# The last stage of a two-layer model: 24 row gathers given at once, and rows fetched back behind the last sequence's gathers

## The chip, the core and the metric

The kernel runs on one core of a Trainium2 chip. The metric is device time in microseconds of one launch. A core has a matrix engine (TensorE, PE in the profile, with its weight loads as PEld), a vector engine (VectorE, DVE), an activation engine (ScalarE, ACT), a general one (GpSimd, POOL) and a queue for transfers (SyncE, SP). Each engine takes its instructions strictly in its own order; between engines they wait on semaphores. Gathers and scatters by an index are issued by POOL, plain transfers by SP (a few by ACT).

## The reference, cut to what matters

The input x has 4 sequences of 1024 tokens of 256 f32. Layer 0 is windowed attention and a top-2-of-8 mixture of SwiGLU experts, layer 1 full attention with a layer norm; they fill the time up to the last stage. That stage is the end of the second mixture, where each expert chooses its tokens:

```python
def _L1_ffn_ref(x, gate_w, experts):            # x: (4, 1024, 256), already normalised
    gate_logits = jnp.einsum('bnd,de->bne', x, gate_w)
    competitive_gates = sinkhorn(gate_logits)   # 8 rounds: over tokens, then over experts
    vals, idx = jax.lax.top_k(jnp.swapaxes(competitive_gates, -1, -2), M)   # M = 128 per expert
    gate_values = jnp.swapaxes(vals, -1, -2)
    routed_indices = jnp.swapaxes(idx, -1, -2)
    b_idx = jnp.arange(B)[:, None, None]
    routed = x[b_idx, routed_indices]
    routed = jnp.transpose(routed, (2, 0, 1, 3))
    outputs = jnp.einsum('ebmd,edf->ebmf', routed, experts)
    outputs = outputs * jnp.transpose(gate_values, (2, 0, 1))[..., None]
    vals_bmed = jnp.transpose(outputs, (1, 2, 0, 3))
    routed_back = jnp.zeros_like(x).at[b_idx, routed_indices].set(vals_bmed)
    return routed_back
```

Its result is added to x. A token can be chosen by several experts; its row is set, not summed, so that one of the experts wins.

## The kernel before, in words

**Which sequence is where.** Sequences 0 to 2 go through the choice of tokens while layer 1's attention still runs; their slots (token, gate) are ready when the last stage begins. Sequence 3 is normalised, gated and chosen in the last stage itself. So the last stage has two strands, whose instructions are laced together by hand.

**Strand one: the experts on sequences 0 to 2.** There are 24 columns, one for each pair of sequence and expert, of 128 slots each. `take_rows` (L1499) gathers the rows of a column from DRAM (`xn_d`) into a tile `xg` (POOL, an indirect transfer; there are 24 buffers). `turned` transposes two columns on PE and copies them out on ACT (`xgT`); four matmuls follow, and ACT scales the result into `yg` (4 buffers), which SP writes to a table `y_d` in DRAM (L1576). `experts_on` (L1536) does this as a generator, `jobs`, two columns at a time, so twelve pairs. It gives ten gathers at first, and then two more in each `turn`, as the pairs go; these are paced, which means that they wait for ACT's newest instruction.

To bring the rows back to their tokens, the kernel finds for each token its row in `y_d`. ACT makes a row of signs for each column (`hot`, `one_sign`), PE adds them up (`sum_signs`), `ranks` turns the sums (ACT copies them to `both`), and `sources` makes the row numbers on DVE (`key`, then `src_row`). `backs` (L1579) then gathers eight tiles of 128 tokens: for sequence 0 they are accumulated into `x` by the transfer itself, for sequences 1 and 2 they land in `yr` and are added on DVE (`add`). `put_on` (L2377) writes the finished `x` tiles of a sequence to the output: sequences 0 and 1 on SP, sequence 2 on SP and ACT.

**Strand two: the choice for sequence 3.** `share_steps` (L1333) is the eight Sinkhorn rounds: DVE sums, PE adds over the partitions, DVE takes the reciprocal (L1350) and scales. A pair of the first strand stands in the order beside these rounds. `choose_parts` (L1364) then finds the 128 best tokens of each expert, eight at a time, in 16 rounds of a maximum and a replacement on DVE (`top_v`, `cur`). After every fourth round a part, a quarter of 32 slots of each expert, is known: `keep` makes `slot_row` (DVE), `slot_tok` and `slot_gate` (ACT) out of a product on PE. `go_on(n)` advances it by n steps.

For each quarter a: `begin` (L2292) gathers its 256 rows into two tiles `xl` (POOL) and has PE spread the tokens; `aim` (L2318) finds on DVE which of the duplicates lose; `make` (L2334) transposes the rows and multiplies them with the experts in strips of 32 slots; `give` (L2354) makes the finished `row` on DVE and scatters it to the output (POOL).

**What sets the order.** `in_line` puts every ACT, DVE and POOL operation of the stage in the order of the program text; PE's order follows `in_turn`, and SP's the text. So the order of the calls in the last stage is the order on each engine, and a waiting instruction holds up everything behind it there. `pair_of_experts` (L2396) is three steps of the choice, one pair of strand one and two rows of signs.

Of the kernel before, what the change touches and what calls it, by code (L numbers as in the profile page):

```python
# [39 lines left out]
def two_layers(  # L40
# [55 lines left out]
    lines = {"scalar": [], "vector": [], "gpsimd": []}  # L96
# [252 lines left out]
    with ExitStack() as lc:  # L349
        wpool = lc.enter_context(tc.tile_pool(name="a0_w", bufs=1))  # L350
        pool = lc.enter_context(tc.tile_pool(name="a0", bufs=2))
# [429 lines left out]
        for i in range(NT + LAG + 2):  # L781
            last, m = i - LAG, i + AHEAD
# [87 lines left out]
    with ExitStack() as lc:  # L870
        wpool = ffn0.enter_context(tc.tile_pool(name="f0_w", bufs=1))
        spool = ffn0.enter_context(tc.tile_pool(name="f0_s", bufs=1))
        pool = ffn0.enter_context(tc.tile_pool(name="f0", bufs=2))
# [383 lines left out]
        for m, (t0, nt, n) in enumerate(order):  # L1257
            ws, b3_t, _ = ahead
# [240 lines left out]
    def take_rows(slots, columns, pool, behind=None):  # L1499

        xgs = []
        for b, n in columns:
            xg = pool.tile([P, D], F32, tag="xg", name="xg", bufs=24)
            got = in_line(
                "gpsimd", nc.gpsimd.indirect_dma_start,
                out=xg[:, :],
                out_offset=None,
                in_=xn_d[b][:, :],
                in_offset=bass.IndirectOffsetOnAxis(ap=slots[2][:, n : n + 1], axis=0),
            )  # L1510
            if behind is not None:
                paced(got.ins, behind)
            xgs.append(xg)
        return xgs

    def turned(xgs, pool, pieces: int = 1):

        ps = one_bank()
        for h, xg in enumerate(xgs):
            for kc in range(2):  # L1520
                c = (2 * h + kc) * P
                turn_on(ps[:, c : c + P], xg[:, kc * P : (kc + 1) * P], ident)
        xgT = pool.tile([P, 4, P], F32, tag="xgT", name="xgT", bufs=3)
        ps = ps.rearrange("p (k t) -> p k t", k=4)
        for k in range(0, 4, 4 // pieces):
            in_line(
                "scalar", nc.scalar.copy,
                xgT[:, k : k + 4 // pieces], ps[:, k : k + 4 // pieces],
            )
        return xgT  # L1530
# [5 lines left out]
    def experts_on(g: int, columns, pool, w_all):  # L1536

        slot_gate = chosen[g, 0][0]
        depth = 10
        xgs = take_rows(chosen[g, 0], columns[:depth], pool)  # L1540

        def turn(m: int):
            xgT = turned(xgs[m : m + 2], pool)
            more = columns[m + depth : m + depth + 2]
            if more:
                xgs.extend(take_rows(chosen[g, 0], more, pool, lines["scalar"][0]))
            return xgT

        ahead = turn(0)
        yield 0  # L1550
        for m in range(0, len(columns), 2):
            xgT = ahead
            if m + 2 < len(columns):
                ahead = turn(m + 2)
                yield m
            ps = one_bank()
            for h in range(2):
                for kc in range(2):
                    mm_on(
                        ps[:, h * D : (h + 1) * D],  # L1560
                        lhsT=xgT[:, 2 * h + kc, :],
                        rhs=w_all[:, (m + h) % E, kc, :],
                        start=(kc == 0),
                        stop=(kc == 1),
                    )
                if h == 0:
                    yield m
            for h in range(2):
                b, e = divmod(m + h, E)
                yg = pool.tile([P, D], F32, tag="yg", name="yg", bufs=4)  # L1570
                in_line(
                    "scalar", nc.scalar.activation,
                    yg, ps[:, h * D : (h + 1) * D], AF.Copy,
                    scale=slot_gate[:, m + h : m + h + 1],
                )
                nc.sync.dma_start(out=slots_of(SEQS[g][b], e, 0, CAP), in_=yg)  # L1576
            yield m

    def backs(b: int, src_row, pool, adds: bool):  # L1579

        rows = []
        for t in range(TB):
            i = b * TB + t
            yr = pool.tile([P, D], F32, tag="yr", name="yr", bufs=2 * TB) if adds else x_t[i]
            in_line(
                "gpsimd", nc.gpsimd.indirect_dma_start,
                out=yr[:, :],
                out_offset=None,
                in_=y_d[b][:, :],
                in_offset=bass.IndirectOffsetOnAxis(ap=src_row[:, t : t + 1], axis=0),  # L1590
                compute_op=ALU.bypass if adds else ALU.add,
            )
            rows.append((x_t[i], yr))
        return rows
# [5 lines left out]
    chosen = {}  # L1600
# [556 lines left out]
    with ExitStack() as lc:  # L2157
# [85 lines left out]
        def sources(both):  # L2243
            key = pool.tile([P, TB, E], F32, tag="key", name="key")
            in_line(
                "vector", nc.vector.tensor_tensor,
                key.rearrange("p t e -> p (t e)"), both[:, TB * E :], both[:, : TB * E], ALU.subtract
            )
            in_line(
                "vector", nc.vector.tensor_tensor,  # L2250
                key, key, expert_no[:, :1].to_broadcast([P, TB, E]), ALU.add,
            )
            src_row = pool.tile([P, TB], I32, tag="src_row", name="src_row")
            in_line("vector", nc.vector.tensor_reduce, src_row, key, AX.X, ALU.max)
            return src_row
# [30 lines left out]
        def go_on(n: int):  # L2286
            for _ in range(n):
                next(choose, None)

        begun, made = {}, {}  # L2290

        def begin(a: int):  # L2292
            slot_tok, slot_row = chosen[1, a][1:]
            xgs = []
            for h in range(2):
                xg = pool.tile([P, 2 * D], F32, tag="xl", name="xl", bufs=6)
                in_line(
                    "gpsimd", nc.gpsimd.indirect_dma_start,
                    out=xg[:, :],
                    out_offset=None,  # L2300
                    in_=xn_d[NB - 1][:, :],
                    in_offset=bass.IndirectOffsetOnAxis(ap=slot_row[:, h : h + 1], axis=0),
                )
                xgs.append(xg)
            ps = one_bank()
            for h in range(2):
                mm_on(
                    ps[:, h * P : (h + 1) * P],
                    lhsT=slot_tok[:, h : h + 1].to_broadcast([P, P]),
                    rhs=ident,  # L2310
                    start=True,
                    stop=True,
                )
            begun[a] = xgs, ps
# [62 lines left out]
        def put_on(b: int, queues):  # L2377
            for t in range(TB):
                i = b * TB + t
                w = queues[t % len(queues)].dma_start(  # L2380
                    out=out_rows[i * P : (i + 1) * P, :], in_=x_t[i]
                )
                tc.add_to_no_dep_group("whole_rows", w.ins)
                for group in groups_out:
                    tc.declare_no_dep(w.ins, group=group, reason="other sequences")

        def begin_ready():
            for a in range(4):
                if (1, a) in chosen and a not in begun:
                    begin(a)  # L2390

        def add(rows):
            for x, yr in rows:
                in_line("vector", nc.vector.tensor_tensor, x, x, yr, ALU.add)
# [1 line left out]
        def pair_of_experts(signs: bool = True):  # L2396
            go_on(3)
            next(jobs, None)
            sum_signs()
            if signs:  # L2400
                one_sign()
            next(jobs, None)
            next(jobs, None)
            if signs:
                one_sign()

        go_on(3)
        sum_signs()
        at = ranks(0)
        go_on(1)  # L2410
        for _ in range(2):
            pair_of_experts()
        backs(0, sources(at), pool, False)
        for _ in range(2):
            pair_of_experts()
        sum_signs()
        at = ranks(1)
        pair_of_experts()
        begin_ready()
        go_on(1)  # L2420
        rows1 = sources(at)
        put_on(0, [nc.sync])
        pair_of_experts()
        aim(0)
        adds1 = backs(1, rows1, pool, True)
        pair_of_experts()
        pair_of_experts()
        make(0)
        begin_ready()
        pair_of_experts(False)  # L2430
        give(0)
        aim(1)
        for _ in jobs:
            pass
        sum_signs()
        make(1)
        at = ranks(2)
        while (1, 2) not in chosen:
            go_on(1)
        begin_ready()  # L2440
        give(1)
        rows2 = sources(at)
        adds2 = backs(2, rows2, pool, True)
        go_on(2)
        aim(2)
        make(2)
        while (1, 3) not in chosen:
            go_on(1)
        begin_ready()
        give(2)  # L2450
        add(adds1)
        put_on(1, [nc.sync])
# [41 lines left out]
```

## Time and profile before

| | |
|---|---|
| three runs | 2206.23, 2200.26, 2199.81 us; median 2200.26 |
| the profiled execution | 2202.66 us, of which the span from the first to the last instruction is 2200.9 |
| mean granted TensorE clock | 0.970 |
| busy share of the span | PE 94%, DVE 61%, ACT 44%, POOL 30% |
| last stage, POOL | 24 gathers `xg`: 14 from 2061.81 us on, pairs at 2085.25, 2093.73, 2102.95, 2107.10 and 2124.48 |
| last stage, POOL, the rest | `x` (accumulating) from 2109.60, `yr` from 2140.92 and 2170.11; `xl` from 2127.05, 2150.91, 2164.91 and 2182.45 |
| last stage, DVE | first maximum of the choice 2095.80; `slot_row` of the quarters 2111.10, 2138.32, 2164.48, 2182.02 |
| last stage, ACT | last `yg` 2159.99 |
| end of the span | 2200.9 |

All times inside the kernel are microseconds from the start of the span, of the profiled execution. In rows of the timeline the first number is the start, the second the duration; what stands in brackets is the idle time of the engine just in front of it and what ended it ("issue": nothing that the profile shows; "remote": a signal that it can't put down to an instruction). SPq is SP's queue of transfers. In rows of waits the three numbers are the total, how often, and the longest. Many helpers record their operations at one line (L103), so rows are told apart by the names of the tiles.

### The profile page before, as it was taken

What the parts mean: (1) busy time and instruction counts of PE and PEld (TensorE: products, weight loads), DVE (VectorE), ACT (ScalarE), POOL (GpSimd) and SP (SyncE); (2) the same over time, 40 slices, a digit from 0 to 9 for tenths busy, and PEclk for the clock granted to TensorE, in tenths of its full rate; (3) what the DMA queues carried; (4) which work ended last, traced back from release to release, by engine and by line L of the source; (5) the groups of instructions that cost most, each with busy time, mean ns of one, the idle gap of its engine ahead of it and who ended that gap; (6) DMA issues with size and microseconds to landing.
All of it is one profiled execution on the core that took longest, in us unless ns stands there. A gap on an engine that the chain in (4) does not pass through costs nothing.

```text
span 2200.9 us, 50595 instructions
## 1 busy us (share of the span) xinstructions
PE 2061.2 (94%) x20050; PEld 1353.7 (62%) x20050; DVE 1333.0 (61%) x2660; ACT 969.6 (44%) x1885; POOL 669.4 (30%) x947
## 2 busy tenths in 40 slices
PE   6999989999999999998899999999999999997674
PEld 4777765556688888874455555555555655554342
DVE  6676654522222222234789787878787878898464
ACT  3554553111122222212156676666666666655351
POOL 2665551243000000012333322314141404033644
PEclk9999999999999999999999999999999999998686
DMA  5111106112266767655162313131313131100344
GB/s 150 53 42 49 54 14 205 37 62 92 73 201 229 232 222 229 211 182 115 50 133 67 79 51 76 49 63 50 78 51 78 51 75 44 51 22 21 101 112 132
DMA packets 205224, 213.68 MB, mean 97 GB/s; under 512 B 87080, under 2 KB 164360, under 8 KB 204988
## 3 DMA queue, kind: packets, MB, share of 16 engines
q1 hardware_dynamic: 181228, 169.00, 27.1%
q0 software_dynamic: 11952, 30.55, 4.9%
q10 hardware_dynamic: 11808, 10.89, 1.4%
q8 instruction: 159, 2.61, 0.5%
q14 instruction: 77, 0.63, 0.1%
HBM read 140.64 MB, written 57.97 MB: 90 GB/s over the span
## 4 chain that ended last, share of the span: by engine, by line
PE 78%; DVE 8%; issue 6%; POOL 3%; DMA 3%; ACT 2%; SPq 1%; ACTq 0%; DVEq 0%; POOLq 0%
PE one L86 36%; PE acc L86 17%; PE two L86 13%; PE two L82 7%; PE misc L82 2%; PE acc L82 2%; DVE tops L1799 2%; DVE tops L1802 1%; POOL xg L103 1%; PE misc L86 1%; POOL yr L2012 1%; DMA yr<-ys_d,slot 1%; DVE top_v L103 1%; DMA w_t<-in_L_ffn_rw_dram 1%; DVE cur L103 1%
## 5 line engine op out<-in xcount | busy, mean ns | idle before, releaser
L1849 ACT ACTIVATE wide<-one 128x512 f32<-128x512 f32 x1024 | 529.6, 603 | 239.4 <-PE one L86 232.8
L1799 DVE TENSOR_REDUCE tops<-two 128x2 f32<-128x1024 f32 x268 | 325.9, 1218 | 84.6 <-PE two L86 79.3
L1802 DVE TENSOR_REDUCE tops<-one 128x1 f32<-128x512 f32 x488 | 311.8, 679 | 0.0
L86 PE MATMUL acc<-wide,v_t 128*32 128x256 f32 x4096 | 276.7, 388 | 0.4 <-issue 0.4
L86 PE MATMUL two<-xbT,w_t 128*128 128x256 f32 (+1 forms) x1280 | 253.6, 356 | 2.0 <-ACT xbT L1186 1.4
L86 PE MATMUL one<-q_st,k_st 64*128 64x512 f32 x1024 | 238.6, 450 | 6.1 <-DVE gates L1324 5.0
L86 PEld LDWEIGHTS two<-xbT,w_t 128*128 128x128 f32 x1280 | 221.6, 190 | 29.5 <-ACT xbT L1186 1.8
L1219 DVE SCALAR_TENSOR_TENSOR glu_b<-two,b_blk,act_b 128x256 f32<-128x256 f32 (+1 forms) x160 | 72.5, 453 | 244.7 <-ACT act_b L1212 244.7
L86 PE MATMUL one<-top_st,minus 64*128 64x512 f32 x1024 | 209.7, 395 | 0.0
L1212 ACT ACTIVATE act_b<-two,b_blk 128x256 f32<-128x256 f32 (+1 forms) x160 | 72.1, 451 | 295.2 <-PE two L86 155.5
L86 PEld LDWEIGHTS acc<-wide,v_t 128*32 128x32 f32 x4096 | 107.7, 109 | 110.8 <-issue 64.0
L86 PE MATMUL one<-k_st,q_st 64*128 64x512 f32 x488 | 168.8, 449 | 3.0 <-DVE ctx L1881 1.2
L86 PEld LDWEIGHTS one<-q_st,k_st 64*128 64x128 f32 x1024 | 101.6, 185 | 95.4 <-ACT wide L1849 35.2
L318 ACT ACTIVATE act<-two,bT 128x512 f32<-128x512 f32 x60 | 41.2, 687 | 264.7 <-PE two L82 259.2
L86 PEld LDWEIGHTS one<-k_st,q_st 64*128 64x128 f32 x488 | 86.4, 184 | 76.9 <-ACT wide L1849 53.3
L2012 POOL DMA_INDIRECT yr<-ys_d,slot x64 | 61.8, 966 | 212.1 <-DMA ys_d<-yb 80.5
L86 PE MATMUL acc<-w_t,glu_b 128*128 128x256 f32 x552 | 125.6, 379 | 0.0
L1269 POOL TENSOR_TENSOR x<-x,sb_b 128x256 f32<-128x256 f32 x32 | 23.3, 727 | 336.2 <-DVE glu_b L1219 336.2
L82 PE MATMUL two<-wide,w_t 128*128 128x512 f32 x256 | 115.1, 603 | 5.8 <-DVE tops L1799 5.0
L648 POOL TENSOR_SCALAR_AFFINE_SELECT pT<-pT 64x512 f32<-64x512 f32 x128 | 84.0, 656 | 115.1 <-ACT pT L638 113.1
L86 PEld LDWEIGHTS acc<-w_t,glu_b 128*128 128x128 f32 x552 | 101.9, 190 | 12.3
L319 DVE SCALAR_TENSOR_TENSOR glu<-two,bT,act 128x512 f32<-128x512 f32 x60 | 44.8, 747 | 102.8 <-ACT act L318 73.4
(395 smaller groups left out, 3341.4 us busy)
## 6 DMA issues: line engine op xcount, KB each, us to landing
w_t<-in_L_ffn_rw_dram SPq DMA_DIRECT2D x120, 512.0 KB
halves<-split SPq DMA_DIRECT2D x64, 256.0 KB
q_st<-halves SPq DMA_DIRECT2D x128, 128.0 KB
k_st<-halves SPq DMA_DIRECT2D x256, 64.0 KB
xb<-xs_d SPq DMA_DIRECT2D x31, 256.0 KB
ys_d<-yb ACTq DMA_DIRECT2D x31, 256.0 KB
xs_d<-zeros SPq DMA_DIRECT2D x5, 1536.0 KB
b_t<-in_L_ffn_rb_dram SPq DMA_DIRECT2D x40, 128.0 KB
```

The lines of the kernel that those rows point to most:

```text
L82: return do(*args, **kw)
L86: done = do(*args, **kw)
L103: done = do(*args, **kw)
L318: nc.scalar.activation(act, ps[0], AF.Silu, bias=bT[0][:, f, e : e + 1])
L319: done = nc.vector.scalar_tensor_tensor(glu[:, f, :], ps[1], bT[1][:, f, e : e + 1], act, ALU.add, ALU.mult)
L648: nc.gpsimd.affine_select(out=part, in_=part, compare_op=ALU.is_ge, fill=0.0, base=0, pattern=[[0, 8], [1, WIN]], channel_multiplier=-1,)
L1212: nc.scalar.activation(act[:, :cols], ps[:, ff * cols : (ff + 1) * cols], AF.Silu, bias=b_blk[0][:, f, n : n + 1],)
L1219: nc.vector.scalar_tensor_tensor(glu[:, f, :cols], ps[:, 512 + ff * cols : 512 + (ff + 1) * cols], b_blk[1][:, f, n : n + 1], act[:, :cols ...
L1799: last = nc.vector.tensor_reduce(tops[:, :, j, kk], whole[0], AX.X, ALU.max)
L1802: last = nc.vector.tensor_reduce(tops[:, hh, j, kk : kk + 1], sc[hh], AX.X, ALU.max)
L1849: newest["scalar"] = nc.scalar.activation(pt[:, hh * 512 : (hh + 1) * 512], sc[hh], AF.Exp).ins
L2012: ga = nc.gpsimd.indirect_dma_start(out=yr[:, :], out_offset=None, in_=ys_d[:, :], in_offset=bass.IndirectOffsetOnAxis(ap=slots[k][:, i : ...
```

## The change

`experts_on` gives all 24 gathers at its start, with no pacing, and `turn` only transposes. `begin_ready`, which began all quarters that were ready, is replaced by `until(a)`, which goes on with the choice until quarter a is known and begins it at once. The calls of the last stage are put in a new order: the row numbers of sequence 0 are found after one pair instead of two, but its rows are fetched back after four pairs and behind the first quarter's `xl` gathers; `aim(0)`, `make(0)` and `give(0)` come earlier against the pairs; the row numbers of sequence 1 are found two pairs after their `ranks` instead of one; `put_on(0)` stands behind one pair more, and `backs(1)` behind the gathers of the second quarter and the scatters of the first. `make(1)` stands in front of the end of the pairs. From the third quarter on, the order is nearly as before.

In the order on the engines this gives: on POOL 24 `xg`, 2 `xl`, 8 `x`, 2 `xl`, 2 scatters, 8 `yr`, then as before. On SP, behind sequence 0's eight `y_d` writes, come four of sequence 1, five tiles of `put_on(0)`, two writes, three tiles, two writes, then sequence 2's eight; before, the eight tiles of `put_on(0)` stood in front of all of sequence 1's and 2's writes.

```diff
@@ experts_on @@
         slot_gate = chosen[g, 0][0]
-        depth = 10
-        xgs = take_rows(chosen[g, 0], columns[:depth], pool)
+        xgs = take_rows(chosen[g, 0], columns, pool)
 
         def turn(m: int):
-            xgT = turned(xgs[m : m + 2], pool)
-            more = columns[m + depth : m + depth + 2]
-            if more:
-                xgs.extend(take_rows(chosen[g, 0], more, pool, lines["scalar"][0]))
-            return xgT
+            return turned(xgs[m : m + 2], pool)
@@ last stage @@
-        def begin_ready():
-            for a in range(4):
-                if (1, a) in chosen and a not in begun:
-                    begin(a)
-
...
+        def until(a: int):
+            while (1, a) not in chosen:
+                go_on(1)
+            begin(a)
+
         go_on(3)
         sum_signs()
         at = ranks(0)
-        go_on(1)
-        for _ in range(2):
+        pair_of_experts()
+        rows0 = sources(at)
+        for _ in range(3):
             pair_of_experts()
-        backs(0, sources(at), pool, False)
-        for _ in range(2):
-            pair_of_experts()
+        until(0)
+        backs(0, rows0, pool, False)
         sum_signs()
         at = ranks(1)
         pair_of_experts()
-        begin_ready()
-        go_on(1)
+        aim(0)
+        pair_of_experts()
         rows1 = sources(at)
+        make(0)
+        pair_of_experts()
         put_on(0, [nc.sync])
-        pair_of_experts()
-        aim(0)
+        until(1)
+        give(0)
         adds1 = backs(1, rows1, pool, True)
         pair_of_experts()
-        pair_of_experts()
-        make(0)
-        begin_ready()
+        aim(1)
         pair_of_experts(False)
-        give(0)
-        aim(1)
+        make(1)
         for _ in jobs:
             pass
         sum_signs()
-        make(1)
         at = ranks(2)
-        while (1, 2) not in chosen:
-            go_on(1)
-        begin_ready()
+        until(2)
         give(1)
         rows2 = sources(at)
         adds2 = backs(2, rows2, pool, True)
         go_on(2)
         aim(2)
         make(2)
-        while (1, 3) not in chosen:
-            go_on(1)
-        begin_ready()
+        until(3)
         give(2)
```

## The prediction

> **What bounds the kernel now.** The page's engine shares come first: PE is busy 94% of the span, but the slices show that this is the mean over stages, and that the last three slices (from 2036 us on) are different. Everything that the diff touches lies there, so the windows of that stretch are the second view.
>
> ```profile
> 2040.00:2080.00 40.00, 25.08 (x122) 13.63 (x122) 21.83 (x61) 11.48 (x22) 27.28 (x46) 0.59 0.41 123
> 2080.00:2120.00 40.00, 28.54 (x139) 16.81 (x138) 28.21 (x65) 23.77 (x36) 16.43 (x14) 0.87 0.32 80
> 2120.00:2160.00 40.00, 28.42 (x159) 18.87 (x160) 19.42 (x42) 15.92 (x29) 18.89 (x19) 0.83 0.53 141
> ```
>
> The columns are the window, its length, and busy time of PE, weight loads, DVE, ACT and POOL, then clock, DMA share and GB/s. No engine is full: DVE has 19.4 of 40 us in the third. Order and waits bind here, so the third view is the waits of DVE and of ACT from 2060 us to the end.
>
> ```profile
> DVE row L103 <- remote: 10.2, 1, 10.2
> DVE slot_row L103 <- PE one L86: 9.5, 2, 7.5
> DVE slot_row L103 <- remote: 6.6, 1, 6.6
> DVE key L103 <- ACT both L103: 5.8, 1, 5.8
> ```
>
> ```profile
> ACT yg L103 <- issue: 18.6, 6, 8.7
> ACT yg L103 <- DMA y_d<-yg: 8.2, 2, 7.6
> ```
>
> Two chains share the stretch. The first is DVE's choosing: the first maximum starts at 2095.80, maxima and replacements go at about 2.54 us a round, and the third quarter's row numbers (slot_row) come at 2164.48. Before that it stands for 5.84 (key of sequence 1), 7.54 (slot_row of the second quarter) and 10.19 us (row of the first quarter). The second chain is the expert pairs, twelve of them, each ended by two yg on ACT: the fourth at 2105.52, the twelfth at 2159.99. Its gaps from there, by the timeline of ACT, are 6.55, 4.15, 14.7, 6.3, 4.4, 4.15, 11.6 and 2.66 us. From 2164.48 to the end at 2200.9 are 36.4 us, in which both programs hold the same instructions in nearly the same order. So the question is when the third quarter's row numbers and the last yg come.
>
> The 14.7 gap is told by the chain of waits:
>
> ```profile
> 2122.58 4.06 DMA x<-y_d,src_row
> 2126.66 0.33 SPq L2380
> 2127.08 0.38 SPq L1576
> 2127.56 4.36 DMA y_d<-yg
> 2132.01 0.47 ACT yg L103
> ```
>
> SP's queue writes sequence 0 out (L2380) as its rows arrive, and sequence 1's first y_d writes stand behind all of it; yg has four buffers, so ACT waits for these writes.
>
> **The change part by part.** *The ten late gathers given at once.* The timeline of POOL:
>
> ```profile
> 2078.26 0.94 POOL L103 DMA_INDIRECT xg<-xn_d,slot_row  x1 [0.30 <-issue]
> 2085.25 0.94 POOL L103 DMA_INDIRECT xg<-xn_d,slot_row  x1 [6.04 <-ACT xgT L103]
> 2086.49 0.95 POOL L103 DMA_INDIRECT xg<-xn_d,slot_row  x1 [0.30 <-issue]
> ```
>
> A gather follows the next at 1.25 us, so ten more take 12.5 us and the burst that starts at 2061.81 ends near 2091.7, not 2079.2. Nobody waits for these rows so early: saved by themselves, 0. What they may cost is the Sinkhorn rounds beside them. Rounds with little wait take 2.1 to 2.6 us (reciprocal to reciprocal, L1350); the two that end at 2075.29 and 2081.69 take 5.04 and 6.40, with DVE waiting 3.5 and 4.9 us for PE, and the second ends 2.5 us after the last gather of the burst. That reads like PE's signals being held while gathers are issued without a pause, from about 10 us into a burst. If all rounds wait until the longer burst is over, the first maximum comes 12.4 us later; if the delay is that of the rows themselves (a cold PE, clock 0.59 there), 0. Below 0 nothing speaks, since the rounds hold the same work. The nearest case is a round at 6.4 us instead of 2.3 for the added stretch, two or three rounds, 7 us for T0; but T0 only reaches the end through DVE's chain, which has slack (next step), while the pairs behind the rounds lose perhaps half. I take 3 us at the end, bounds 0 to 12.4.
>
> The Trainium skill ("DMA: Bandwidth & Descriptors", the section on the anatomy of a GpSimd DMA) gives each such transfer a fixed 2.0 us and its bytes at 436 GB/s, which for 131 KB is an estimated 2.3 us, against the 1.25 us pitch above; by it the burst would last until about 2102 and the cost be nearly twice mine, some 2194 in all. The row decides for the pitch.
>
> *The DVE waits.* The key of sequence 1 moves two pairs behind its ranks, about 8 us, against a wait of 5.84: gone. The row of the first quarter gets make(0) one pair earlier, and stands right behind slot_row of the second quarter; most of its 10.19 goes (PE had its product at 2150.3, and the signal came at 2155.11, 2.0 us after the burst of yr and xl gathers). The 7.54 in front of slot_row goes with the SP wait, since PE's products in front of it stood behind that yg. Sum 5.84 + 7.54 + 10.19 + 2.00 (in front of slot_row 12) = 25.6 us, bounds 15 to 25.6. DVE alone would have the third quarter's row numbers near 2139. It is no longer what is late; the pairs are.
>
> *The pairs.* On SP, in the new order, four of sequence 1's y_d writes stand in front of put_on(0), two behind its fifth row, two behind its eighth. On POOL two gathers of the first quarter (xl) stand in front of the eight accumulating ones, and wait for slot_row of the first quarter, 2111.10 in this trace. Accumulating ones then go at 1.85 us from 2113.8 instead of 2109.60, 4.2 us later, and the last lands near 2131 (4 us each). The seventh pair's writes so go at about 2126, the eighth's near 2132, landing in 1.9 to 4.4 us: the ninth pair is free, the tenth waits until some 2136. Five gaps with no such stall (6.55, 4.15, 6.3, 4.4, 4.15) have a mean of 5.1 us; eight at that are 41, so the last yg comes at 2146.5, with 2 us for the tenth pair's buffers 2148.5, against 2159.99. Gain 11.5, say 12. Bounds: 8, if the 8.7 us wait in front of the eleventh pair (it stands behind make(0) and the burst of yr gathers) comes back behind make(1) by half; 16, if the gaps are those of 4.2 to 4.4. Of the 10 xg gathers taken from POOL's later queue, the last two stood at 2124.48, in front of xl; that is 2.5 us of POOL off, and not on a path.
>
> *The end.* 36.4 us behind slot_row 12 stay: two xl, the scatters, eight yr, the fourth quarter, the adds and the writes have the same order on POOL and SP. Bounds -2 to +2, since the row numbers of the fourth quarter wait 6.62 us there for a PE that had finished at 2175.75, behind the third burst, and this may fall otherwise.
>
> Sum: profiled execution 2202.66, less 12, plus 3: 2193.7. The profiled one is 2.4 us above the median of the runs shown, 2200.26, so 2191. Of this kernel a measurement can tell about 0.3%, 6.6 us, from no change; the gain is 9.
>
> **The rivals.** *The long burst costs nothing.* If the slow rounds come from the cold clock alone, the 3 us go and the pairs run at their short gaps: 2202.66 - 16 - 2.4 = 2184. For it: the accumulating burst of 2109.60 to 2124 held no signal, and early rounds were slow with the clock at 0.5. Against: both slow rounds and the first yg (7.94 us, "remote") were released right behind the last gather.
>
> *The burst holds the rounds in full, and the gain is used up.* T0 comes near 2107 and the first yg near 2094 instead of 2081.81; three gaps of 6 make the fourth pair 2112, 6.3 late. DVE with its slack is at 2150, the last yg at 2154.5: 2202.66 - 12 + 6.3 - 2.4 = 2194.6, about the line of what can be told; 2200 if the wait in front of the eleventh pair is met again.
>
> *Slower: the hold comes in each burst.* The place is POOL's queue from xl of the first quarter on. With T0 at 2107 slot_row comes at 2122.5, and 2 + 8 + 2 gathers go unbroken for 19.8 us, until 2142.3, where before the eight went ahead of it without need of DVE. If this burst holds as the first, signals come at 2144.5, four pairs at 4.2 follow (2161.3), and the 6.3 us of the third burst of before is met in the middle of them: last yg 2167.6, 7.6 behind now, so 2208, and to 2212 with PE at half clock behind each stop (2165.7 to 2193 has 0.5). It decides from a last yg later than 2166.6, and needs T0 beyond some 2105 and a hold in the accumulating burst too. For it: three of the four bursts show a release just behind them. Against: the accumulating one did not.
>
> **How the numbers follow.** The forecast has 0.42, of which 0.10 lies above 2193.7; no cost 0.12; full hold 0.18; slower 0.28. So faster by over 0.3% is 0.44, within it 0.28, slower 0.28. The likeliest case reaches from 2187 (gain 16 at a cost of 3) to 2198 (gain 8 at a cost of 6). The range to hold the time 8 times in 10 goes from 2184 to 2210, leaving out a little below and the worst of the slow case.
>
> **What would show it.** Right: 24 gathers at 1.25 us from 2062 to 2092; the first maximum at 2096 to 2103; no wait of key; four y_d writes ahead of the rows of sequence 0 on SP; the eleventh yg without its 8.7 us; last yg at 2148 to 2152; slot_row of the third quarter 4 us behind it; then 36 us. Wrong: a first maximum behind 2105; waits called remote of over 5 us behind the accumulating gathers; a new wait of ACT's yg for y_d of 5 us or more; or a last part that is not 36 us long.

## The result, and the profile after

The changed kernel takes 2212.14 us (median of 20 runs, 2199.76 to 2220.74) beside 2200.72 of the kernel before (20 runs, 2195.48 to 2206.68). The ratio is 1.0049, 95% interval 1.0034 to 1.0064: slower by half a per cent, where 2191 was forecast. The profiled execution took 2217.37 us, with a span of 2215.6.

The windows of the last stage of the changed kernel, with the columns as before:

```profile
2040.00:2080.00 40.00, 24.54 (x140) 13.40 (x139) 21.98 (x58) 14.17 (x28) 28.80 (x55) 0.62 0.35 109
2080.00:2120.00 40.00, 19.62 (x76) 11.66 (x75) 14.48 (x50) 10.15 (x14) 13.27 (x14) 0.62 0.21 63
2120.00:2160.00 40.00, 30.90 (x201) 19.58 (x200) 30.19 (x55) 26.12 (x43) 20.68 (x17) 0.93 0.55 136
2160.00:2216.00 56.00, 25.87 (x195) 14.48 (x193) 25.66 (x61) 7.99 (x20) 23.21 (x24) 0.65 0.38 119
```

The window from 2080 to 2120 us is the one that went wrong: DVE is busy for 14.5 us instead of 28.2, ACT for 10.2 instead of 23.8. The third window is the fuller one now (DVE 30.2 instead of 19.4). So something new stops the stage early, and the new order does make the middle denser. The waits of DVE and ACT from 2060 us on name the stop:

```profile
DVE rc L1350 <- remote: 17.5, 2, 11.2
DVE slot_row L103 <- PE one L86: 16.8, 2, 11.7
DVE slot_row L103 <- remote: 6.7, 1, 6.7
```

```profile
ACT yg L103 <- remote: 22.1, 1, 22.1
ACT yg L103 <- issue: 17.0, 6, 4.2
```

In the kernel before, the same two views have these lines for rc and for the first yg:

```profile
DVE rc L1350 <- PE two L86: 8.4, 2, 4.9
ACT yg L103 <- remote: 7.9, 1, 7.9
```

The 5.8 us of key, the 10.2 of row and the 8.2 of yg for its y_d writes are gone, as the forecast had it. In their place stand 17.5 us in front of the Sinkhorn reciprocal rc (instead of 8.4) and 22.1 in front of the first yg (instead of 7.9), both "remote". The timeline of DVE and of POOL puts them beside the gathers:

```profile
2081.08 0.21 DVE L1350 RECIPROCAL rc<-one 128x8 f32<-128x8 f32 x1 [3.76 <-PE two L86]
2093.82 0.21 DVE L1350 RECIPROCAL rc<-one 128x8 f32<-128x8 f32 x1 [11.22 <-remote]
2101.60 0.21 DVE L1350 RECIPROCAL rc<-one 128x8 f32<-128x8 f32 x1 [6.27 <-remote]
```

```profile
2067.43 1.13 POOL L103 DMA_INDIRECT xg<-xn_d,slot_row  x1 [6.16 <-PE misc L82]
...
2096.50 0.95 POOL L103 DMA_INDIRECT xg<-xn_d,slot_row  x1 [0.30 <-issue]
```

The 24 gathers last from 2067.43 to 2097.45, 1.25 us apart. Three rounds in a row are stopped in that time; the last goes on 4.2 us behind the end of the burst, and then rounds take 2.6 to 3.5 us again. The product that the second of them waits for is written down as started on PE at 2082.74, so that DVE had it 11 us after PE began. The page "Perfetto Trace Analysis" of the Trainium skill says (in its part on the lifecycle of an instruction) that the profile's end of a PE instruction is an estimate and not observed. So the trace can't tell whether PE finished late or its signal came late; what counts here is when DVE and ACT could start. "Held" below means no more than that.

Of the 14.7 us between the spans of the two profiled executions, 5.6 lie in front of the stage (the first xg at 2067.43 instead of 2061.81). A second profile of the same changed program (r_after below) has it at 2061.81 again, so these are not of the change. The rest is 13.5 us more between the first xg and the first maximum (47.5 instead of 34.0), 4.9 less from there to the third quarter's row numbers (63.8 instead of 68.7), and 0.4 more from there to the end.

### The profile page after: what moved, and what is told of

Read it like the earlier page. It is cut to its first block, busy times and chain, and to the rows that moved or that the text cites. A ratio compares the mean times of both kernels' runs of the same rounds, so it can differ in the third digit from the quotient of the medians.

```text
span 2215.6 us, 50582 instructions
## 1 busy us (share of the span) xinstructions
PE 2067.6 (93%) x20050; PEld 1356.7 (61%) x20050; DVE 1332.4 (60%) x2660; ACT 969.4 (44%) x1885; POOL 670.3 (30%) x947
## 5 line engine op out<-in xcount | busy, mean ns | idle before, releaser
L86 PEld LDWEIGHTS acc<-wide,v_t 128*32 128x32 f32 x4096 | 107.6, 109 | 110.6 <-issue 63.8
L86 PEld LDWEIGHTS acc<-w_t,glu_b 128*128 128x128 f32 x552 | 101.9, 190 | 12.3
```

The costliest lines, as they stand in the source:

```text
L86: done = do(*args, **kw)
```

## The experiments

The theory that the experiments start from, H: a long, unbroken series of gathers issued by GpSimd holds PE's products back from DVE and ACT, and the change made the series longer. Against it stand the new order itself (O), the bytes that land (B), and the mere number of gathers (N).

The experiments ran in five jobs on four chips: e1 to e4 on one, r_after and e5 on a second, e1b to e4b on a third, e6 and e7 on the first of these again, e6b and r2_after on a fourth. Which chip gave the result above isn't known. The kernel before ran in each job as the yardstick (16 to 35 runs, beside 4 to 12 of a variant), and a ratio is always one to its runs in the same job. It isn't exactly the quotient of the two medians beside it; the two differ by up to 0.0014.

| run | edit, against the kernel named | before, same chip | this | ratio (95%) |
|---|---|---|---|---|
| e1_paced | changed, pacing of before | 2186.18 | 2180.27 | 0.9977 (0.9964 to 0.9991) |
| e2_all24 | before, all 24 at once | 2186.18 | 2184.80 | 0.9992 (0.9980 to 1.0005) |
| e3_rate | changed, spaced xg | 2186.18 | 2182.82 | 0.9991 (0.9978 to 1.0003) |
| e4_plain | changed, plain loads on SP | 2186.18 | 2183.36 | 0.9991 (0.9976 to 1.0006) |
| r_after | changed, unedited | 2200.38 | 2202.42 | 1.0019 (1.0003 to 1.0035) |
| e5_depth4 | changed, paced, four at first | 2200.38 | 2194.76 | 0.9988 (0.9972 to 1.0003) |
| e1b_paced | as e1 | 2199.99 | 2195.97 | 0.9984 (0.9971 to 0.9998) |
| e2b_all24 | as e2 | 2199.99 | 2210.34 | 1.0039 (1.0024 to 1.0054) |
| e3b_rate | as e3 | 2199.99 | 2191.84 | 0.9949 (0.9931 to 0.9968) |
| e4b_plain | as e4 | 2199.99 | 2190.00 | 0.9944 (0.9924 to 0.9964) |
| e6_all_rate | changed, spaced xg and yr | 2183.87 | 2184.91 | 1.0002 (0.9989 to 1.0016) |
| e7_old_rate | before, all 24 at once, spaced | 2183.87 | 2189.62 | 1.0016 (1.0003 to 1.0030) |
| e6b_all_rate | as e6 | 2198.91 | 2186.65 | 0.9947 (0.9928 to 0.9966) |
| r2_after | changed, unedited | 2198.91 | 2203.37 | 1.0023 (1.0010 to 1.0035) |

To read the traces side by side, the last stage is cut in three: A from the last gates (the start of Sinkhorn) to the first maximum, B from there to the third quarter's slot_row, C from there to the end of the span. All are differences of starts in the timeline of DVE. "Held" is the longest wait for rc.

| trace | kernel before there | A | B | C | held |
|---|---|---|---|---|---|
| before | 2200.7 | 29.0 | 68.7 | 36.5 | 4.9 |
| changed | 2200.7 | 42.5 | 63.8 | 36.8 | 11.2 |
| r_after | 2200.4 | 40.2 | 57.8 | 36.3 | 13.2 |
| r2_after | 2198.9 | 40.2 | 58.5 | 36.6 | 11.0 |
| e2b_all24 | 2200.0 | 40.3 | 64.6 | 36.4 | 11.8 |
| e1b_paced | 2200.0 | 27.2 | 65.3 | 36.5 | 5.5 |
| e5_depth4 | 2200.4 | 20.2 | 68.3 | 36.6 | 0.9 |
| e3b_rate | 2200.0 | 20.9 | 66.2 | 36.7 | 0.9 |
| e4b_plain | 2200.0 | 20.2 | 63.2 | 39.7 | 0.9 |
| e6b_all_rate | 2198.9 | 21.0 | 61.7 | 37.4 | 1.0 |
| e2_all24 | 2186.2 | 21.6 | 64.0 | 34.3 | 1.9 |
| e1_paced | 2186.2 | 20.4 | 57.9 | 34.0 | 0.9 |
| e3_rate | 2186.2 | 21.0 | 57.9 | 34.1 | 0.9 |
| e4_plain | 2186.2 | 21.4 | 57.1 | 37.1 | 1.9 |
| e6_all_rate | 2183.9 | 21.2 | 55.8 | 37.3 | 1.8 |
| e7_old_rate | 2183.9 | 21.0 | 65.4 | 34.1 | 0.9 |

**e1_paced: the new order without the long burst.**

```diff
-        xgs = take_rows(chosen[g, 0], columns, pool)
+        depth = 10
+        xgs = take_rows(chosen[g, 0], columns[:depth], pool)
         def turn(m: int):
-            return turned(xgs[m : m + 2], pool)
+            xgT = turned(xgs[m : m + 2], pool)
+            more = columns[m + depth : m + depth + 2]
+            if more:
+                xgs.extend(take_rows(chosen[g, 0], more, pool, lines["scalar"][0]))
+            return xgT
```

> The changed kernel with the gathers of before: ten at first, then two per pair, paced behind ACT; the new order of the last stage stays. Theory H (the longer unbroken burst of gathers holds PE's signals): from the first xg to the first maximum 34 us as before (47.5 in the changed kernel), first yg 20 us behind the first xg (34.2), and the whole near 2195, since the new order by itself gained 4.4 us between the first maximum and the end. Rival O (the new order of the calls makes the choice start late, or gains nothing): 45 us or more to the first maximum, or 34 us and a whole of 2200 or more.

**e2_all24: the long burst without the new order.** The kernel before, with the two lines of the change in `experts_on` alone.

> The kernel before, with only one edit: all 24 gathers given at once, no pacing; the old order stays. Theory H: 45 to 50 us from the first xg to the first maximum, and since the old order gets nothing back, 2209 to 2214. Rival O: 34 us, 2200 within 3.

**e3_rate: the burst longer, but not back to back.**

```diff
                 paced(got.ins, behind)
+            rest = pool.tile([P, 512], I32, tag="rest", name="rest", bufs=1)
+            in_line("gpsimd", nc.gpsimd.iota, rest, pattern=[[1, 512]], base=0, channel_multiplier=0)
             xgs.append(xg)
```

> The changed kernel with a GpSimd iota of 128x512 behind each of the 24 gathers, so that they go at some 2 us instead of 1.25: the burst is longer (about 48 us instead of 30) but not back to back. Theory H in its form 'the rate is the cause' (the accumulating gathers at 1.85 us held no signal): no wait of rc above 4 us, first maximum 32 to 36 us behind the first xg, whole 2195 to 2203. Rival N (the number of gathers under way, or the length of the burst, is the cause): the rounds wait until the 48 us are over, first maximum 50 to 60 us, whole 2220 or more.

**e4_plain: the same bytes by another issuer.** The loads bring rows 128e to 128e+127 instead of the chosen ones, so this kernel leaves out the gather by index.

```diff
-            got = in_line(
-                "gpsimd", nc.gpsimd.indirect_dma_start,
...
-            )
+            e = n % E
+            nc.sync.dma_start(out=xg, in_=xn_d[b][e * P : (e + 1) * P, :])
```

> The changed kernel with the 24 gathers by index replaced by 24 plain loads of the same size on SP (rows 128e to 128e+127 of the sequence instead of the chosen ones, so the experts work on other rows). Theory H (GpSimd's issuing is the cause): no wait of rc above 3 us, first maximum 30 to 34 us behind the first load, whole 2190 to 2198. Rival B (the bytes and the landing of 24 tiles are the cause): waits of rc as in the changed kernel while the loads land, though shorter, and a whole of 2205 or more.

These four ran on one chip, and there the expectation for e2 failed: 21.6 us in A and not the 40 or more that H asked for, with 24 gathers 1.25 us apart just as in the changed kernel. Its rounds:

```profile
2071.33 0.21 DVE L1350 RECIPROCAL rc<-one 128x8 f32<-128x8 f32 x1 [0.91 <-PE one L86]
2074.71 0.21 DVE L1350 RECIPROCAL rc<-one 128x8 f32<-128x8 f32 x1 [1.86 <-PE one L86]
2077.05 0.21 DVE L1350 RECIPROCAL rc<-one 128x8 f32<-128x8 f32 x1 [0.82 <-PE one L86]
```

No wait called remote is in any trace of that chip, and the kernel before was itself 14.5 us faster there. The times that the four expectations name were worked out for the chip of the result and are all too long here; so are their first maxima (25.4 us behind the first xg in e1 and 26.0 in e3, where 34 and 32 to 36 were expected). Either H was wrong, or the hold is there on some chips and not on others. So the next job took the changed kernel unedited, and one with a short series.

**r_after, r2_after: the changed kernel, unedited.**

> The changed kernel once more, unedited, beside the kernel before. The first four experiments showed no wait called remote at all, and the kernel before at 2186 instead of 2200.7, so the hold of PE's signals seems not to be there in every place where the program runs. Theory C (the hold belongs to the chip or session, not to the program): where the kernel before takes some 2186, the changed one shows no rc wait above 3 us, 25 to 28 us from the first xg to the first maximum, and 2180 to 2185, so faster by 0.1 to 0.3%; where the kernel before takes some 2200, 47 us and 2209 to 2215. Rival P (the hold belongs to this program's instruction layout, the four variants having changed it by chance): 45 us or more and 8 us or more behind the kernel before, wherever it runs.

> The changed kernel, unedited, once more. Theory C: if the kernel before takes some 2186 here, no wait of rc above 4 us, the first maximum 26 to 28 us behind the first xg, and 0.996 to 0.999; if it takes some 2200, 45 to 48 us to the first maximum and 1.001 to 1.006. Rival P: the same 45 us or more in either case.

Both met chips on which the kernel before takes some 2200, and both times the hold was there: A 40.2 us, and 1.0019 and 1.0023 (2202.42 us in the first, where 2209 to 2215 was expected). The regression is smaller than the 1.0049 of the first chip, but each interval lies above one.

**e5_depth4: four gathers at first.** As e1, with depth = 4.

> The new order with pacing, four gathers at first instead of ten, then two per pair. Theory H: with a burst of 8 (four, and two pairs in the first turns) no rc wait above 3 us, the first maximum 24 to 27 us behind the first xg, whichever the place, and 1 to 3 us less than the kernel with ten (0.996 to 0.998 of the kernel before where that takes 2186; 0.994 or less where it takes 2200). Rival G (the rows come too late with so few ahead): the transposes wait for xg, yg pairs 2 to 5 later by 4 us each, the same as the kernel before or slower.

On the chip of r_after, a series of at most eight with pauses has A at 20.2 us, as low as on the chip without a hold: 20 us less than the changed kernel, and H's expectation. But B is 68.3, and the tenth and eleventh yg pairs come 12.3 and 10.0 us behind those in front of them. The last four late gathers now stand on POOL behind the eight accumulating ones, from 2127.13 on, and PE's transposes for the tenth pair wait for their rows:

```profile
2131.51 1.09 PE L86 MATMUL one<-ident,xg 128*128 128x128 f32 x4 [4.04 <-DMA xg<-xn_d,slot_row]
```

So rival G is part of it, at the tenth pair and not at the second to fifth; what keeps the eleventh the trace doesn't say. Only 7.7 us of the 20 reach the end; the ratio is 0.9988, within noise of one, where 0.994 or less was expected, and no better than the 0.9984 of ten at first (e1b below).

**e1b, e2b, e3b, e4b: the first four on a chip with the hold.**

> The new order with ten gathers at first and the rest paced, once more, to have it on a chip where PE's signals are held (the kernel before at some 2200 there). Theory H there: as in the kernel before, two rounds are held, the first maximum is 33 to 35 us behind the first xg (45 to 47 with all 24 at once, 25 with four), no gain from the new order that the later bursts don't take back in part: 0.993 to 0.998 of the kernel before. Rival O (the new order itself costs time): 1.000 or more. If the kernel before takes some 2186, 0.997 again and no wait called remote.

> The old order with all 24 gathers at once, once more. Theory H where signals are held: 44 to 48 us from the first xg to the first maximum and 1.004 to 1.008 of the kernel before, since nothing is given back. Rival O: 34 us and 1.000. If the kernel before takes some 2186: 0.999 again.

> The changed kernel with a GpSimd iota behind each of the 24 gathers (1.7 us apart, as the first run of it showed), once more. Theory H, form 'rate': where signals are held no more than one round waits over 3 us, the first maximum 26 to 34 us behind the first xg, 0.993 to 0.998 of the kernel before. Rival N (a long series of gathers, at whatever rate): 45 us or more to the first maximum, and 1.002 or more. If the kernel before takes some 2186: 0.999 again.

> The changed kernel with plain loads on SP in place of the 24 gathers (the experts work on other rows), once more. Theory H (gathers that GpSimd issues): where signals are held, no rc wait above 3 us, first maximum 25 to 28 us behind the gates, later waits behind the yr gathers as in the changed kernel; 0.993 to 0.998 of the kernel before. Rival B (the bytes that land): rc waits of 5 us or more while the loads land, and 1.000 or more. If the kernel before takes some 2186: 0.999 again.

This decides it. First the rounds of e2b, the same program as e2, in the timeline of DVE:

```profile
2073.67 0.21 DVE L1350 RECIPROCAL rc<-one 128x8 f32<-128x8 f32 x1 [1.46 <-PE one L86]
2082.80 0.21 DVE L1350 RECIPROCAL rc<-one 128x8 f32<-128x8 f32 x1 [7.61 <-remote]
2096.13 0.21 DVE L1350 RECIPROCAL rc<-one 128x8 f32<-128x8 f32 x1 [11.81 <-remote]
2098.41 0.21 DVE L1350 RECIPROCAL rc<-one 128x8 f32<-128x8 f32 x1 [0.75 <-PE one L86]
```

One program, two chips: A 21.6 and 40.3 us, ratio 0.9992 and 1.0039. The long burst alone, in the old order, costs 0.39%; theory P (an accident of this program's layout) and rival O fall. Then e3b, where the gathers take longer, 2061.57 to 2101.70, but are 1.71 us apart:

```profile
2061.57 1.12 POOL L103 DMA_INDIRECT xg<-xn_d,slot_row  x1 [6.17 <-PE misc L82]
2062.72 0.58 POOL L103 IOTA rest<- 128x512 int32 x1
2063.46 0.97 POOL L103 DMA_INDIRECT xg<-xn_d,slot_row  x1 [0.17 <-issue]
```

```profile
2072.37 0.21 DVE L1350 RECIPROCAL rc<-one 128x8 f32<-128x8 f32 x1 [0.90 <-PE one L86]
2074.81 0.21 DVE L1350 RECIPROCAL rc<-one 128x8 f32<-128x8 f32 x1 [0.93 <-PE two L86]
2076.88 0.21 DVE L1350 RECIPROCAL rc<-one 128x8 f32<-128x8 f32 x1 [0.54 <-PE one L86]
```

No round waits a microsecond, A is 20.9, and the kernel is at 0.9949, faster than both. Number and length (N) are not the cause; the rate is, and 0.46 us more between two gathers is enough (whether it is the time or the other instruction between them that counts was not told apart). The bytes (B) are not either: e4b, where SP issues the loads, has A 20.2 and 0.9944, and there the transfers moved 220 GB/s from 2065 to 2075 us, against 105 in e2b from 2070 to 2080. But its loads are given within 12 us, less than the 13 us that the series in e2b goes before the first long stop, and they read rows in one piece and not by an index; a longer series of them was not run. Pacing with ten at first (e1b) leaves two slow rounds, as in the kernel before: 32.2 us from the first xg to the first maximum (33 to 35 expected) and 0.9984, a smaller gain than the 0.993 to 0.998 expected.

**e6_all_rate, e6b_all_rate: the yr gathers spaced too.**

```diff
+            if adds:
+                rest = pool.tile([P, 512], I32, tag="rest", name="rest", bufs=1)
+                in_line(
+                    "gpsimd", nc.gpsimd.iota, rest, pattern=[[1, 512]], base=0, channel_multiplier=0
+                )
             rows.append((x_t[i], yr))
```

> The changed kernel with the iota behind each of the 24 gathers and behind each of the 16 yr gathers too (1.7 us apart instead of 1.25; the accumulating ones stay at 1.85). Theory H where the kernel before takes some 2200: the wait called remote in front of the fourth quarter's slot_row (6.5 us in seven of seven traces with held signals) falls below 3, the pairs beside the first yr series go at 4 to 5 us, and the whole is 0.988 to 0.994 of the kernel before. Rival Z (what holds these is the transfers, not the rate of issuing): the remote wait stays at 6 us or grows with the series by 3.6, and 0.995 to 0.998. Where the kernel before takes some 2186, 0.996 to 1.000, since 3.6 us of later yr gathers are paid for nothing.

> The changed kernel with the iota behind each of the 24 xg and the 16 yr gathers, once more, to meet a chip where signals are held (the kernel before at some 2200). Theory H there: the remote wait in front of the fourth quarter's slot_row below 3 us (6.5 in every trace with held signals so far), third quarter's slot_row 58 to 62 us behind the first maximum (66.2 without the yr spacing), 0.986 to 0.993 of the kernel before. Rival Z (the order is worth no more): 64 us or more and 0.994 to 0.998. If the kernel before takes some 2186: 1.000 again.

The fourth quarter's slot_row in e3b and in e6b, both where signals are held:

```profile
2171.33 0.16 DVE L103 CAST slot_row<-one 128x2 int32<-128x2 f32 x1 [6.54 <-remote]
```

```profile
2157.46 0.16 DVE L103 CAST slot_row<-one 128x2 int32<-128x2 f32 x1 [0.36 <-PE one L86]
```

The remote wait of 6.5 us is gone with the spacing, in this series as in the first, and B goes from 66.2 to 61.7. The changed kernel without spacing (r2_after) ran on the same chip in the same job: A 40.2 against 21.0, ratio 1.0023 against 0.9947. The fourth and fifth rounds there, first in r2_after, then in e6b:

```profile
2081.82 0.21 DVE L1350 RECIPROCAL rc<-one 128x8 f32<-128x8 f32 x1 [8.30 <-remote]
2094.44 0.21 DVE L1350 RECIPROCAL rc<-one 128x8 f32<-128x8 f32 x1 [11.04 <-remote]
```

```profile
2071.75 0.21 DVE L1350 RECIPROCAL rc<-one 128x8 f32<-128x8 f32 x1 [1.01 <-PE two L86]
2073.81 0.21 DVE L1350 RECIPROCAL rc<-one 128x8 f32<-128x8 f32 x1 [0.54 <-PE one L86]
```

But the 0.9947 is no better than e3b's 0.9949 on another chip: part of what spacing gives is paid for by the longer series, C 37.4 instead of 36.7 here, 37.3 instead of 34.1 where nothing is held. On the chip without a hold the version is at 1.0002. The expected 0.986 to 0.993 was not met; only the mechanism was.

**e7_old_rate: what the new order is worth.** As e2, with e3's iota.

> The kernel before, in its old order, with all 24 gathers given at once and the iota behind each: what the new order is worth by itself, when the gathers hold nothing. The forecast's step said that the new order takes 12 us from the way between the first maximum and the third quarter's row numbers (68.7 us in the kernel before). Expected if that was right: the first maximum 26 us behind the first xg, 67 to 70 us from there to the third quarter's row numbers, and some 8 to 12 us slower than the new order with the same iota (e3: 66.2 us where signals are held). Rival W (the new order gains little): within 4 us of it.

On the chip without a hold B is 65.4 us in the old order (67 to 70 expected) and 57.9 in the new (e3): 7.5 us. The ratios, 1.0016 and 0.9991, each 0.0013 either way, put the new order at 0.25%, some 5.5 us: less than the 8 to 12 expected and more than the 4 of rival W. e1 against its yardstick, where both pace their gathers, gives 0.23%, some 5 us. So the order is a gain. The spacing itself isn't free where nothing is held: the old order with all 24 at once has 0.9992 without the iota (e2) and 1.0016 with it.

## Why the prediction was wrong

**The burst.** The count and the pitch were right: 24 gathers, 1.25 us apart, 30.0 us. The failing step is the next one: "I take 3 us at the end, bounds 0 to 12.4". The run that has this term alone is e2b, the long burst in the old order: 1.0039, some 8.6 us. For the delay of the first maximum the step had 7 us; the three traces of the changed kernel have 13.5, 11.3 and 11.2 (47.5, 45.3 and 45.2 from the first xg, against 34.0). So the step had the right mechanism and took about a third of its price, by two wrong readings. It took the rounds to go on slowly, at 6.4 us each, in the added stretch; two of them stop for 6 to 13 us each. And it let DVE's slack take most of the delay: in e2b A is 11.3 us longer than in the kernel before and B only 4.1 shorter. The pairs were to lose perhaps half, though the same hold keeps the first yg as well, so that both chains move: the first yg is 34.2 us behind the first xg, and 27.6 and 26.9 in the other two traces, against 20.0. Beside that the 3 us hid a cost that was already there: on the chips with a hold A is 29.0 in the kernel before and 20.2 to 21 when the gathers are few or spaced, so its burst of 14 cost 8 us of the 29 already. The step priced the longer series from that row without asking what the row would be with no series held.

**The DVE waits.** 25.6 us of waits were to go, the third quarter's row numbers then waiting for the pairs. key, row and yg's wait for y_d went as said. (The rounds of the choice go at 2.59 us in the rows and not at 2.54; no term uses it.) New waits of 5.1 and 11.7 us stand in front of slot_row in the profiled execution, the second with the yr gathers (2157 to 2166.8) in front of it. B fell by 4.9 us there and by 10.9 and 10.2 in the other two traces.

**The pairs.** A mean gap of 5.1 us and 12 us of gain, 8 to 16, were said. From the fourth yg pair to the last the changed kernel takes 45.5 us in r_after and 46.2 in r2_after instead of 54.5: 9.0 and 8.3 less. In the profiled execution it is 50.6, 3.9 less. The order by itself gives 4.5 to 6.6 of that: with all 24 gathers given first, the old order takes 49.9 in e2, 51.9 in e7 and 52.0 in e2b, and the new one 45.4 in e3. At the end of the span it gives 5 to 5.5 us (e1; e7 and e3). So SP's writes went as the step said and the 14.7 gap is gone (put_on(0) stands behind two pairs more in the new text, not one), but the term of 12 was about twice too large. In r_after the largest gaps are others: the seventh pair comes 8.6 us behind the sixth, with ranks(1) in between, and the ninth 7.9 us behind the eighth, with make(0) in between and ACT waiting 3.9 us for PE; the second is the same on the chip without a hold.

**The end.** 36.4 us from the third quarter's row numbers were said, and 36.3 to 36.8 measured in the three traces of the changed kernel.

**The sum by what was measured.** In r_after, on a chip like the first: 11.3 lost in front of the first maximum, 10.9 gained behind it, 0.2 gained at the end. That is 0.2 us more than the profiled execution of before, whose chip is another; its own ratio is 1.0019, some 4 us. At the end, measured one by one, the forecast's two terms are 8.6 us instead of 3 and 5 to 5.5 instead of 12. From 2200.7 that makes an estimated 2204, or 1.0015: near the 1.0019 and 1.0023 of the two later chips, and some 8 us short of the 2212.14 of the first. A time of 2204 would have lain inside the forecast's 2184 to 2210 by luck, since the two errors would have been the same.

**The rivals.** "The long burst costs nothing" is false where it was forecast, and true on one chip that the forecast didn't know of. The cold clock that it names isn't the cause: in r_after the granted clock is 0.50 from 2066 to 2072 us, and the round from 2067.98 to 2070.25 takes 2.27 us. "Held in full" had the size right, with the first maximum at about 2107 (2107.07 and 2105.79), and its 2194.6 wrong. "Slower" asked for a hold in the accumulating series as well. Its point of decision, a last yg later than 2166.6, was passed in the profiled execution (2175.22) and not in r_after and r2_after (2160.62 and 2160.08), and the time lies at its upper end; but the accumulating series, 1.85 us apart, isn't where it came from: the gaps of the pairs beside it and just behind it, 9.2, 4.4 and 7.9 us, are those of e1 on the chip without a hold (9.2, 4.4 and 7.9). That the changed kernel scatters over 21 us, and that the first chip gave 1.0049 and two others 1.0019 and 1.0023, is not explained.

**What stays open.** Why PE's products come late on these chips beside GpSimd's gathers at 1.25 us, and not at 1.71, wasn't tried by itself, and no run shows what makes the one chip different; it had no hold in either of its two jobs. The unedited change did not meet the chip without a hold, so its ratio there isn't known; e1 to e4, which share its order or its burst, are 0.998 to 0.999 there.

## What to carry to other kernels

A row that shows a wait beside a series of gathers has a price for the series that is already there, and a change that lengthens the series should be priced from the case with none: here 20 to 21 us in front of the first maximum where the gathers are few or spaced, 29 with 14 at once, 40 with 24. Giving independent gathers early was not free here, because work on the path stood beside them; spacing them on the issuing engine (0.46 us each) made an order that lost 0.2 to 0.5% gain 0.51% (with the yr gathers spaced too, 1.0023 and 0.9947 on one chip). Where nothing was held, the same spacing gained nothing. And when a variant shows no effect at all, look first at what the yardstick took: the same program had the hold on one chip and not on another.

## What the runs showed of the hardware

- Gathers that GpSimd issues back to back, 1.25 us apart, kept PE's products from DVE and ACT from some 10 to 13 us into the series until 2 to 4 us behind its end, on the chips where the kernel before takes some 2200 us (with 24 gathers two waits of 6 to 13 us each, with 14 waits of up to 5.5). Gathers 1.71 us apart did not, and neither did plain loads issued by SP, 24 of them within 12 us.
- On the chip where it takes some 2185 us the same programs (e1 and e2) showed none of it, and the last stage from the third quarter's row numbers on was 2.1 to 2.6 us shorter in e1, e2 and e3 (34.0 to 34.3 us instead of 36.4 to 36.7).
- The price on POOL of one xg or yr gather given back to back was 1.25 us; the accumulating ones took 1.85. The page "DMA: Bandwidth & Descriptors" of the Trainium skill gives a fixed 2.0 us for one transfer (its section on the anatomy of a GpSimd DMA) and puts most of it down to completion, not to setup. The prediction read it as the pitch of a series, and these rows show that it is not that.
